# Queries of an attention block by seven quarter products: Strassen's algorithm for a second projection of a Trainium2 kernel

## The chip, the core and the metric

The kernel runs on one core of one Trainium2 chip. The metric is the device time in microseconds (us) of one execution. A core has five engines that run their own instruction queues in order and meet at semaphores: TensorE (PE, matrix products, with its weight loads shown as PEld), VectorE (DVE), ScalarE (ACT), GpSimd (POOL) and SyncE (SP, which issues DMAs). [...] All data here is 32-bit float, and each product that the program asks for is two matmul instructions and two weight loads in the trace.

## What is computed

One transformer block with adaptive layer norm, for two batches of 1024 tokens, 256 wide. The attention has 16 heads of 128, rotary positions and a causal mask; the second half is a gated feed-forward layer with dequantized weights.

```python
h = _layernorm(x) * (1 + ca) + sa
def proj(W, bias): return (h @ W + bias).reshape(b, n, 16, 128).transpose(0, 2, 1, 3)
q, k, v = proj(Wq, bq) * scale, proj(Wk, bk), proj(Wv, bv)
q, k = apply_rotary(pos, q), apply_rotary(pos, k)     # t*cos + rotate_half(t)*sin
sim = where(causal, -big, einsum('bhid,bhjd->bhij', q, k))
out = einsum('bhij,bhjd->bhid', softmax(sim), v)
x = x + ga * (out @ Wo + bo)
h = _layernorm(x) * (1 + cb) + sb
x = x + gb * down(silu(gate(h)) * up(h))
```

The projections q, k and v are each [1024 x 256] times [256 x 2048] per batch. The scale is folded into the softmax.

## The kernel before, in words

**Units.** The work is cut into 32 units, one for each batch b, group g of two heads, and head h in the group. Unit n is even for the first head of a group and odd for the second. A unit has eight turns i, one for each tile of 128 queries. The loop over units and turns writes the order of every queue out by hand: no scheduler moves anything, so each engine meets its instructions in the order of the program.

**One turn.** In turn i of unit n the program issues, in this order: the output projection of an earlier unit (`shared_out`, L622 to L634: one product "py" on PE, then an addition to x on DVE, L632); the scores of query tile i against (i+1)*128 keys (L542, "ps" on PE), then on DVE the mask and the row maximum (L545); the DVE transposition of the probabilities of the turn before (`turned`, L576, with DMAs after turns 3 and 7); the exponential on ACT (L562); `release()`, which issues the second halves of rotations that were begun in the turn before; then the projections that this turn has been given, the products of probabilities and values of the unit before (L603, "po" on PE, in turns 0, 6 and 7), and `extras`, where single jobs are placed by unit and turn.

**Queries and keys.** `project_qk` (L490 to L521) makes 512 tokens of one head: two products of 512 columns that add up in a PSUM bank, one for each half of the 256 inputs. Then come the rotation's parts: two ACT instructions read the bank crosswise into r1 (L511), POOL multiplies r1 by the sine table (L512); in the next turn DVE computes (bank + bias) * cosine (L515) and POOL adds r1 (L518). It is called in turns 1, 3, 4 and 5 of each unit for the next unit: query block 0, key block 0, query block 1, key block 1.

**Values.** From group 2 of the first batch on, 14 groups in all, `value_step` (L453 to L488) makes the values of both heads of a group from seven products of quarters instead of eight (Strassen's algorithm). The quarters are 512 tokens by 128 inputs, and 128 inputs by the 128 columns of one head. POOL forms sums of the token quarters once for each batch (`token_sum`) and, for each group, four sums of the weight quarters, in place and in one small tile (`weight_sums`, L440 to L451). Each product lies in one PSUM bank; ACT copies two of the seven to "snap" tiles, DVE adds five to snap tiles or values, and POOL adds two more times. Steps 1 to 3 are in turns 0 and 2 of an odd unit (for the next group), steps 4 to 7 in turns 0, 2 and 3 of the even unit that follows.

**Buffers.** Two PSUM banks ("ps_a") serve all projections in turn, one bank serves py, two pairs of banks serve the scores. Queries, keys, values and each of the weight tiles have two buffers, r1 has two.

Of the kernel before, what the change touches and what calls it, by code (L numbers as in the profile page):

```python
# [23 lines left out]
HG = 2  # L24
# [3 lines left out]
QB = 512  # L28
# [9 lines left out]
def adaln_block(ctx: ExitStack, tc: tile.TileContext, a, cos_d, sin_d, out):  # L38
    nc = tc.nc
    pool = lambda name, bufs, **k: ctx.enter_context(tc.tile_pool(name=name, bufs=bufs, **k))  # L40

    const = pool("const", 1)
# [4 lines left out]
    ps_a = pool("ps_a", 2, space=PSUM)  # L47
# [35 lines left out]
    def warm_up(tiles):  # L83
# [22 lines left out]

    modT = const.tile([P, 4, KC, B], F32, name="modT")
    gate = {
        (n, b): const.tile([P, D], F32, name=f"g{n}{b}") for n in ("a", "b") for b in range(B)
    }  # L110
    bo_bc = const.tile([P, D], F32, name="bo_bc")
    bvacc = const.tile([P, D], F32, name="bvacc")
# [33 lines left out]

    def gate_rows(n):

        for b in range(B):
            row = grow_d["ab".index(n), b : b + 1, :]  # L150
            nc.sync.dma_start(gate[n, b], row.to_broadcast([P, D]))
# [51 lines left out]
    wpool = pool("w", 2)  # L203
    vpool = pool("v", 2)
    qkpool = pool("qk", 2)
# [3 lines left out]
    tpool = pool("t", 1)  # L209
# [176 lines left out]
    gbo = {}  # L386

    def bias_row():

        pb = ps_a.tile([P, 512], F32, tag="a", name="pbias")  # L390
        nc.tensor.matmul(pb[:, :D], ones, bvacc, start=True, stop=True)
        nc.vector.tensor_tensor(bo_bc, pb[:, :D], bo_bc, ALU.add)
        for b in range(B):
            gbo[b] = const.tile([P, D], F32, name=f"gbo{b}")
            nc.gpsimd.tensor_tensor(gbo[b], gate["a", b], bo_bc, ALU.mult)

    def add_bias(b, t):
# [3 lines left out]
    weights = {}  # L401
# [21 lines left out]
    tT = {}  # L423
# [13 lines left out]
        }[n]  # L437
        nc.gpsimd.tensor_tensor(tT[b, n], x0, x1, ALU.subtract)

    def weight_sums(b, g, n):  # L440

        w = weights[b, g]["v"]
        a11, a12, a21, a22 = (w[:, k, ts(h, DH)] for h in range(HG) for k in range(KC))
        if n == 0:
            s2 = tpool.tile([P, DH], F32, tag="ws", name=f"ws_{b}{g}")
            wsum[b, g] = (a21, s2, a11, a12)
            nc.gpsimd.tensor_tensor(a11, a11, a21, ALU.subtract)
            nc.gpsimd.tensor_tensor(s2, a22, a11, ALU.subtract)
        else:
            nc.gpsimd.tensor_tensor(a21, a21, a22, ALU.add)  # L450
            nc.gpsimd.tensor_tensor(a12, a12, wsum[b, g][1], ALU.subtract)  # L451

    def value_step(b, g, step):  # L453
        w = weights[b, g]["v"]
        quarter = lambda k, blk: hT[b, blk][:, k, :]
        if step == 1:
            vs[b, g] = vpool.tile([P, NT, HG * DH], F32, tag="v", name=f"v_{b}{g}")
            for n in (1, 2):
                snap[n] = tpool.tile([P, QB], F32, tag=f"s{n}", name=f"snap{n}_{b}{g}")
        part = lambda h, blk: vs[b, g][:, ts(blk, QB // P), ts(h, DH)]  # L460
        tiles = lambda t: t.rearrange("p (t d) -> p t d", d=DH)

        def product(tokens, wq):
            bank = ps_a.tile([P, 512], F32, tag="a", name=f"pv{step}_{b}{g}")
            for r in range(QB // P):
                nc.tensor.matmul(bank[:, ts(r, P)], tokens[:, ts(r, P)], wq, start=True, stop=True)  # L466
            return bank

        add = lambda eng, to, x0, x1: eng.tensor_tensor(to, x0, x1, ALU.add)  # L469
        if step == 1:  # L470
            nc.scalar.copy(snap[1], product(quarter(0, 0), w[:, 0, ts(0, DH)]))
        elif step == 2:
            bank = product(quarter(1, 0), w[:, 1, ts(0, DH)])
            add(nc.vector, part(0, 0), tiles(bank), tiles(snap[1]))
        elif step == 3:
            add(nc.vector, snap[1], product(tT[b, 2], wsum[b, g][1]), snap[1])
        elif step == 4:
            bank = product(quarter(1, 1), wsum[b, g][3])
            add(nc.vector, part(0, 1), tiles(bank), tiles(snap[1]))
        elif step == 5:  # L480
            nc.scalar.copy(snap[2], product(tT[b, 1], wsum[b, g][0]))  # L481
            add(nc.gpsimd, part(0, 1), part(0, 1), tiles(snap[2]))
        elif step == 6:
            add(nc.vector, snap[1], product(tT[b, 3], wsum[b, g][2]), snap[1])
            add(nc.gpsimd, part(1, 1), tiles(snap[1]), tiles(snap[2]))
        else:
            bank = product(tT[b, 4], w[:, 1, ts(1, DH)])
            add(nc.vector, part(1, 0), tiles(bank), tiles(snap[1]))  # L488

    def project_qk(u, s, n):  # L490

        b, g, h = u
        head = g * HG + h
        if n == 0:
            qks[u, s] = qkpool.tile([P, S], F32, tag=f"{s}T", name=f"{s}T_{b}{g}{h}")
        dst = qks[u, s]
        pq = ps_a.tile([P, 512], F32, tag="a", name=f"p{s}_{b}{g}{h}{n}")
        for k in range(KC):
            nc.tensor.matmul(  # L499
                pq,  # L500
                weights[b, g][s][:, k, ts(h, DH)],
                hT[b, n][:, k, :],
                start=(k == 0),
                stop=(k == KC - 1),
            )
        c = (R_BQ if s == "q" else R_BK) + head
        sl, half = ts(n, QB), DH // 2

        r1 = rot.tile([P, QB], F32, tag="r1", name=f"r1_{s}{b}{g}{h}{n}")
        for to, of in ((slice(0, half), slice(half, DH)), (slice(half, DH), slice(0, half))):  # L510
            nc.scalar.activation(r1[to], pq[of], AF.Identity, bias=cols[of, c : c + 1])  # L511
        nc.gpsimd.tensor_tensor(r1, r1, sin_t[:, sl], ALU.mult)  # L512

        def rest():
            nc.vector.scalar_tensor_tensor(  # L515
                dst[:, sl], pq, cols[:, c : c + 1], cos_t[:, sl], ALU.add, ALU.mult
            )
            nc.gpsimd.tensor_tensor(dst[:, sl], dst[:, sl], r1, ALU.add)  # L518


        held.append(rest)  # L521
# [232 lines left out]
    N = len(units)  # L754

    def extras(n, i):
# [8 lines left out]
            gate_b()  # L765
        if n == 6 and i == 3:
            gate_b_turn()
        if n == 7 and i == 3:
            gate_rows("b")

        if n in (2, 15) and i in (0, 1, 3):
            for m in {0: (1, 2), 1: (3,), 3: (4,)}[i]:
                token_sum(n // 15, m)
        if n > 2 and n % 2 and i in (0, 3) and n + 1 < N:
            weight_sums(*units[n + 1][:2], i // 3)

        if n == 2 and i == 7:
            ffn_scale_load()
# [38 lines left out]
        if n == 20:  # L817
            add_bias(1, i)

    filler = (0, 1, 3, 4, 5, 6)  # L820

    def shared_out(s, late=False):
# [3 lines left out]
    with tc.manual_schedule():  # L826
# [52 lines left out]
        for n, u in enumerate(units):  # L879
            b, g, h = u  # L880
            prev = units[n - 1] if n else None
            nxt = units[n + 1] if n + 1 < N else None
            nb, ng = (b, g + 1) if g + 1 < NG else (b + 1, 0)
            more = nb < B
            for i in range(NT):

                shared_out(8 * n + i - 13)
                if owed:
                    owed.pop()()
                ps, nmax = score(u, i)  # L890
                if n > 2 and h == 0 and i == 3:
                    value_step(b, g, 7)
                if i >= 1:
                    turned(u, i - 1)
                elif prev:
                    turned(prev, NT - 1)
                expo(u, i, ps, nmax)
                release()
                if i in (1, 3, 4, 5) and nxt:
                    project_qk(nxt, *{1: ("q", 0), 3: ("k", 0), 4: ("q", 1), 5: ("k", 1)}[i])  # L900
                if i in (6, 7) and prev:
                    values(prev, 1, 4 * (i - 6), 4 * (i - 5))
# [12 lines left out]
                if n == 0 and i in (6, 7):  # L915
                    project_v(0, 1, 2 * (i - 6))
                if not nxt and i in filler:
                    hidden(0, 0, filler.index(i), late=False, hold=True)

                if prev and i == (0 if n > 2 else 2):  # L920
                    values(prev, 0, 0, 4)
                extras(n, i)
                if i == 7 and h == 1:
                    if more:
                        load_out(nb, ng)
                    if n + 3 < N:
                        load_proj(*units[n + 3][:2])
# [122 lines left out]
```

## Time and profile before

| what | us |
|---|---|
| median of 3 runs | 1061.07 (1060.88 to 1061.3) |
| the profiled execution | 1061.52 |
| its span, from the first to the last instruction | 1059.7 |
| PE busy (share of the span) | 1055.0 (100%) |
| DVE busy | 701.0 (66%) |
| ACT busy | 491.3 (46%) |
| POOL busy | 468.5 (44%) |
| granted TensorE clock, mean | 1.000 |

"Busy" is the union of an engine's instructions in the profiled execution. Matmuls are pipelined, so the records of neighbours overlap; what one costs in a stream is read from start to start in the timeline. The trace names instructions by line, engine, operation and tiles ("qT<-pq,cols,cos_t" writes qT from pq, cols and cos_t). A number of microseconds in square brackets is idle time of the engine before an instruction, with what released it.

### The profile page before, as it was taken

What the parts mean: (1) busy time and instruction counts of PE and PEld (TensorE: products, weight loads), DVE (VectorE), ACT (ScalarE), POOL (GpSimd) and SP (SyncE); (2) the same over time, 40 slices, a digit from 0 to 9 for tenths busy, and PEclk for the clock granted to TensorE, in tenths of its full rate; (3) what the DMA queues carried; (4) which work ended last, traced back from release to release, by engine and by line L of the source; (5) the groups of instructions that cost most, each with busy time, mean ns of one, the idle gap of its engine ahead of it and who ended that gap; (6) DMA issues with size and microseconds to landing.
All of it is one profiled execution on the core that took longest, in us unless ns stands there. A gap on an engine that the chain in (4) does not pass through costs nothing.

```text
span 1059.7 us, 13263 instructions
## 1 busy us (share of the span) xinstructions
PE 1055.0 (100%) x3834; PEld 638.4 (60%) x3834; DVE 701.0 (66%) x1523; ACT 491.3 (46%) x930; POOL 468.5 (44%) x461
## 2 busy tenths in 40 slices
PE   9999999999999999999999999999999999999998
PEld 5655566566666665665666666666565666555747
DVE  5667776777777776766676666666777866545331
ACT  5644444454445454444554444454454554562110
POOL 5755464645353554855644544434444544200100
PEclk9999999999999999999999999999999999999999
DMA  5466646666565646565565656454555657423201
GB/s 191 91 173 161 155 112 153 148 148 150 125 157 117 147 112 155 112 152 120 117 148 113 147 113 152 107 144 97 144 112 128 144 132 171 107 59 71 70 0 40
DMA packets 68379, 132.34 MB, mean 125 GB/s; under 512 B 19366, under 2 KB 23476, under 8 KB 68308
## 3 DMA queue, kind: packets, MB, share of 16 engines
q1 hardware_dynamic: 66060, 126.17, 50.6%
q10 hardware_dynamic: 2168, 5.20, 1.5%
q8 instruction: 31, 0.51, 0.2%
q14 instruction: 40, 0.33, 0.1%
q0 software_dynamic: 80, 0.13, 0.1%
HBM read 25.52 MB, written 2.10 MB: 26 GB/s over the span
## 4 chain that ended last, share of the span: by engine, by line
PE 99%; DVE 0%; issue 0%; POOL 0%; POOLq 0%
PE po L603 23%; PE ps L542 23%; PE py L629 10%; PE pq L499 10%; PE pk L499 10%; PE pv L466 8%; PE pgu L658 7%; PE pd L716 2%; PE pv L411 1%; PE pd_0w L716 1%; PE pd_1w L716 1%; PE warm_ps L85 0%; PE ptx_a L254 0%; PE pd L705 0%; PE pm L122 0%; DVE wupT L318 0%
## 5 line engine op out<-in xcount | busy, mean ns | idle before, releaser
L562 ACT ACTIVATE p<-ps,nmax 128x128 f32<-128x128 f32 (+7 forms) x256 | 190.3, 743 | 353.9 <-DVE nmax L545 353.6
L542 PE MATMUL ps<-kT,qT 128*128 128x512 f32 (+3 forms) x768 | 289.6, 486 | 0.0
L603 PE MATMUL po<-pT,v 128*128 128x512 f32 (+3 forms) x768 | 263.7, 486 | 0.2 <-DMA pT<-t 0.2
L545 DVE CUSTOM_DVE_ANT_0 ps<-ps,mask 128x128 f32<-128x128 f32 (+7 forms) x256 | 195.1, 762 | 100.5 <-PE ps L542 100.1
L632 DVE SCALAR_TENSOR_TENSOR x<-py,rden,x 128x256 f32<-128x256 f32 x256 | 122.2, 479 | 179.7 <-PE py L629 176.3
L603 PEld LDWEIGHTS po<-pT,v 128*128 128x128 f32 x768 | 143.6, 190 | 122.5 <-issue 93.5
L576 DVE STREAM_TRANSPOSE t<-p 128x128 f32<-128x128 f32 (+7 forms) x256 | 197.9, 773 | 5.3 <-DMA pT<-t 3.0
L542 PEld LDWEIGHTS ps<-kT,qT 128*128 128x128 f32 x768 | 145.8, 190 | 77.4 <-issue 63.4
L512 POOL TENSOR_TENSOR r_q<-r_q,sin_t 128x512 f32<-128x512 f32 x64 | 82.4, 1287 | 162.4 <-ACT r_q L511 161.0
L629 PE MATMUL py<-wo,o 128*128 128x256 f32 x512 | 151.8, 381 | 0.3 <-DVE x L632 0.3
L629 PEld LDWEIGHTS py<-wo,o 128*128 128x128 f32 x512 | 90.0, 191 | 77.5 <-issue 49.1
L499 PE MATMUL pq<-hT,wq 128*128 128x512 f32 x256 | 120.5, 593 | 0.0
L499 PE MATMUL pk<-hT,wk 128*128 128x512 f32 x256 | 120.3, 592 | 0.0
L512 POOL TENSOR_TENSOR r_k<-r_k,sin_t 128x512 f32<-128x512 f32 x64 | 81.7, 1277 | 47.0 <-ACT r_k L511 46.8
L518 POOL TENSOR_TENSOR kT<-kT,r_k 128x512 f32<-128x512 f32 x64 | 81.2, 1269 | 42.2 <-DVE kT L515 36.4
L511 ACT ACTIVATE r_q<-pq,cols 64x512 f32<-64x512 f32 x128 | 87.6, 684 | 23.5 <-PE pq L499 19.9
L518 POOL TENSOR_TENSOR qT<-qT,r_q 128x512 f32<-128x512 f32 x64 | 81.8, 1278 | 27.1 <-DVE qT L515 24.6
L511 ACT ACTIVATE r_k<-pk,cols 64x512 f32<-64x512 f32 x128 | 87.6, 684 | 10.7 <-PE pk L499 7.0
L499 PEld LDWEIGHTS pk<-hT,wk 128*128 128x128 f32 x256 | 47.5, 190 | 41.4 <-issue 34.9
L499 PEld LDWEIGHTS pq<-hT,wq 128*128 128x128 f32 x256 | 46.1, 190 | 32.8 <-issue 30.3
L611 ACT COPY o<-po 128x512 f32<-128x512 f32 x64 | 37.3, 582 | 59.5 <-PE po L603 59.5
L469 POOL TENSOR_TENSOR v<-v,snap 128x512 f32<-128x512 f32 x14 | 17.7, 1265 | 93.2 <-ACT snap L481 93.2
(135 smaller groups left out, 967.5 us busy)
## 6 DMA issues: line engine op xcount, KB each, us to landing
pT<-t SPq DMA_DIRECT2D x512, 128.0 KB, 2.4
pT<-t SPq DMA_DIRECT2D x512, 64.0 KB, 2.0
wq<-in_Wq SPq DMA_DIRECT2D x16, 256.0 KB, 3.1
wk<-in_Wk SPq DMA_DIRECT2D x16, 256.0 KB, 4.1
wv<-in_Wv SPq DMA_DIRECT2D x16, 256.0 KB, 4.1
wo<-in_Wo SPq DMA_DIRECT2D x16, 256.0 KB, 3.0
out<-yo SPq DMA_DIRECT2D x15, 128.0 KB, 1.7
x<-in_x ACTq DMA_DIRECT2D x4, 256.0 KB, 3.1
```

The source lines that it names most:

```text
L466: nc.tensor.matmul(bank[:, ts(r, P)], tokens[:, ts(r, P)], wq, start=True, stop=True)
L499: nc.tensor.matmul(pq, weights[b, g][s][:, k, ts(h, DH)], hT[b, n][:, k, :], start=(k == 0), stop=(k == KC - 1),)
L511: nc.scalar.activation(r1[to], pq[of], AF.Identity, bias=cols[of, c : c + 1])
L512: nc.gpsimd.tensor_tensor(r1, r1, sin_t[:, sl], ALU.mult)
L518: nc.gpsimd.tensor_tensor(dst[:, sl], dst[:, sl], r1, ALU.add)
L542: nc.tensor.matmul(ps[:, c:e], qT[:, ts(i, P)], kT[:, c:e], start=True, stop=True)
L545: nc.vector.tensor_tensor_reduce(ps[:, :L], ps[:, :L], mask[:, NT - 1 - i :, :].rearrange("p t k -> p (t k)"), -SCALE, FLT_MAX, ALU.add, A ...
L562: nc.scalar.activation(p[:, :L], ps[:, :L], AF.Exp, bias=nmax, scale=-1.0, accum_out=dens[u][:, i : i + 1])
L576: nc.vector.transpose(t32[blk][:, :, j, : i + 1, :].rearrange("p c k b -> p k c b"), p[:, : (i + 1) * P].rearrange("p (k c a) -> p k c a", ...
L603: nc.tensor.matmul(po[:, off * P :], vs[b, g][:, k, ts(h, DH)], pT[:, off:, :, k, :], start=(k == 0), stop=(k == last),)
L629: nc.tensor.matmul(py[:, :D], outs[u][:, ts(t, P)], weights[b, g]["o"][:, h, :], start=True, stop=True)
L632: nc.vector.scalar_tensor_tensor(x[b][:, t, :], py[:, :D], rdens[u][:, t : t + 1], x[b][:, t, :], ALU.mult, ALU.add)
```

## The change

For the same 14 groups, queries are made by the seven quarter products too. `value_step` becomes `set_step`, which serves both: an even unit n > 2 makes the values of its own group, an odd unit n > 2 the queries of both heads of the next group. One step is in each of turns 0, 1, 2, 4, 5, 6 and 7, after the exponential. `project_qk` stays for keys (turns 3 and 5) and for the first units.

A query quarter is finished in the query tile itself, in SBUF. The rotation (now a function of its own, `rotary`) is then applied in place: it is put in a list `due` by the step that completes a quarter, begun in the next turn after `release()`, and its second half, DVE and POOL, is released in the turn after that. Its lines are those of L506 to L521; where its source was a PSUM bank, it is now a part of the query tile. Quarters are completed in steps 2, 5, 6 and 7.

The weight sums are issued at the end of turns 0 and 2 of each such unit, behind everything else that the turn gives to POOL but `extras`. Queries have three buffers. For the room, the gate rows of the second half go into a weight buffer (and are loaded in unit 30 instead of 7), and the bias rows are kept in place of two others.

```diff
     def gate_rows(n):
+        if n == "b":
+            t = wpool.tile([P, KC, HG * DH], F32, tag="wq", name="gb")
+            for b in range(B):
+                gate["b", b] = t[:, b, :]
...
+        gbo.update({0: bvacc, 1: bo_bc})
         for b in range(B):
-            gbo[b] = const.tile([P, D], F32, name=f"gbo{b}")
             nc.gpsimd.tensor_tensor(gbo[b], gate["a", b], bo_bc, ALU.mult)
...
-    def value_step(b, g, step):
-        w = weights[b, g]["v"]
+    due = []
+
+    def set_step(b, g, name, step):
+        w = weights[b, g][name]
...
+        if name == "q" and step in (1, 6):
+            h = step // 6
+            qks[(b, g, h), "q"] = qkpool.tile([P, S], F32, tag="qT", name=f"qT_{b}{g}{h}", bufs=3)
...
+            part = lambda h, blk: qks[(b, g, h), "q"][:, ts(blk, QB)]
...
         def product(tokens, wq):
...
+                nc.tensor.matmul(bank, wq, tokens, start=True, stop=True)
             return bank
 
+        def done(h, blk):
+            if name == "q":
+                due.append(lambda: rotary((b, g, h), "q", blk, part(h, blk)))
+
         if step == 1:
             nc.scalar.copy(snap[1], product(quarter(0, 0), w[:, 0, ts(0, DH)]))
         elif step == 2:
             bank = product(quarter(1, 0), w[:, 1, ts(0, DH)])
             add(nc.vector, part(0, 0), tiles(bank), tiles(snap[1]))
+            done(0, 0)
         elif step == 3:
+            add(nc.vector, snap[1], product(tT[b, 2], s2), snap[1])
         elif step == 4:
+            bank = product(quarter(1, 1), s4)
             add(nc.vector, part(0, 1), tiles(bank), tiles(snap[1]))
         elif step == 5:
+            nc.scalar.copy(snap[2], product(tT[b, 1], s1))
             add(nc.gpsimd, part(0, 1), part(0, 1), tiles(snap[2]))
+            done(0, 1)
         elif step == 6:
+            add(nc.vector, snap[1], product(tT[b, 3], s3), snap[1])
             add(nc.gpsimd, part(1, 1), tiles(snap[1]), tiles(snap[2]))
+            done(1, 1)
         else:
             bank = product(tT[b, 4], w[:, 1, ts(1, DH)])
             add(nc.vector, part(1, 0), tiles(bank), tiles(snap[1]))
+            done(1, 0)
...
-        if n == 7 and i == 3:
+        if n == 30 and i == 3:
             gate_rows("b")
...
-        if n > 2 and n % 2 and i in (0, 3) and n + 1 < N:
-            weight_sums(*units[n + 1][:2], i // 3)
...
+    STEPS = {0: (1,), 1: (2,), 2: (3,), 4: (4,), 5: (5,), 6: (6,), 7: (7,)}
...
-                if n > 2 and h == 0 and i == 3:
-                    value_step(b, g, 7)
...
                 expo(u, i, ps, nmax)
                 release()
-                if i in (1, 3, 4, 5) and nxt:
+                while due:
+                    due.pop(0)()
+
+                setted = n > 2 and (not h or more) and ((nb, ng, "q") if h else (b, g, "v"))
+                if setted and i in STEPS:
+                    for step in STEPS[i]:
+                        set_step(*setted, step)
+                if i in (1, 3, 4, 5) and nxt and (i % 2 == 1 and i > 1 or n < 3):
                     project_qk(nxt, *{1: ("q", 0), 3: ("k", 0), 4: ("q", 1), 5: ("k", 1)}[i])
...
-                if n > 2 and (h == 0 or more) and i in (0, 2):
-                    vg = (nb, ng) if h else (b, g)
-                    for step in {(1, 0): (1, 2), (1, 2): (3,), (0, 0): (4, 5), (0, 2): (6,)}[h, i]:
-                        value_step(*vg, step)
...
                 if prev and i == (0 if n > 2 else 2):
                     values(prev, 0, 0, 4)
+                if setted and i in (0, 2):
+                    weight_sums(*setted, i // 2)
                 extras(n, i)
```

More of the change, by code (lines that the diff above doesn't have):

```diff
@@ L108, in adaln_block @@
     gate = {
-        (n, b): const.tile([P, D], F32, name=f"g{n}{b}") for n in ("a", "b") for b in range(B)
+        ("a", b): const.tile([P, D], F32, name=f"ga{b}") for b in range(B)
     }
@@ L438, in token_sum, with weight_sums @@
         nc.gpsimd.tensor_tensor(tT[b, n], x0, x1, ALU.subtract)
-    def weight_sums(b, g, n):
-        w = weights[b, g]["v"]
+    def weight_sums(b, g, name, n):
+        w = weights[b, g][name]
         a11, a12, a21, a22 = (w[:, k, ts(h, DH)] for h in range(HG) for k in range(KC))
         if n == 0:
-            s2 = tpool.tile([P, DH], F32, tag="ws", name=f"ws_{b}{g}")
-            wsum[b, g] = (a21, s2, a11, a12)
+            s2 = tpool.tile([P, DH], F32, tag="ws", name=f"ws{name}_{b}{g}")
+            wsum[b, g, name] = (a21, s2, a11, a12)
             nc.gpsimd.tensor_tensor(a11, a11, a21, ALU.subtract)
@@ L450, in weight_sums @@
             nc.gpsimd.tensor_tensor(a21, a21, a22, ALU.add)
-            nc.gpsimd.tensor_tensor(a12, a12, wsum[b, g][1], ALU.subtract)
-    def value_step(b, g, step):
-        w = weights[b, g]["v"]
+            nc.gpsimd.tensor_tensor(a12, a12, wsum[b, g, name][1], ALU.subtract)
+    due = []
+    def set_step(b, g, name, step):
+        w = weights[b, g][name]
         quarter = lambda k, blk: hT[b, blk][:, k, :]
         if step == 1:
-            vs[b, g] = vpool.tile([P, NT, HG * DH], F32, tag="v", name=f"v_{b}{g}")
+            if name == "v":
+                vs[b, g] = vpool.tile([P, NT, HG * DH], F32, tag="v", name=f"v_{b}{g}")
@@ L458, in value_step @@
             for n in (1, 2):
-                snap[n] = tpool.tile([P, QB], F32, tag=f"s{n}", name=f"snap{n}_{b}{g}")
-        part = lambda h, blk: vs[b, g][:, ts(blk, QB // P), ts(h, DH)]
-        tiles = lambda t: t.rearrange("p (t d) -> p t d", d=DH)
-        def product(tokens, wq):
-            bank = ps_a.tile([P, 512], F32, tag="a", name=f"pv{step}_{b}{g}")
-            for r in range(QB // P):
-                nc.tensor.matmul(bank[:, ts(r, P)], tokens[:, ts(r, P)], wq, start=True, stop=True)
-            return bank
+                snap[n] = tpool.tile([P, QB], F32, tag=f"s{n}", name=f"snap{name}{n}_{b}{g}")
@@ new lines, in set_step @@
+        if name == "q" and step in (1, 6):
+            h = step // 6
+            qks[(b, g, h), "q"] = qkpool.tile([P, S], F32, tag="qT", name=f"qT_{b}{g}{h}", bufs=3)
+        if name == "v":
+            part = lambda h, blk: vs[b, g][:, ts(blk, QB // P), ts(h, DH)]
+            tiles = lambda t: t.rearrange("p (t d) -> p t d", d=DH)
+        else:
+            part = lambda h, blk: qks[(b, g, h), "q"][:, ts(blk, QB)]
+            tiles = lambda t: t
+        def product(tokens, wq):
+            bank = ps_a.tile([P, 512], F32, tag="a", name=f"p{name}{step}_{b}{g}")
+            if name == "v":
+                for r in range(QB // P):
+                    nc.tensor.matmul(
+                        bank[:, ts(r, P)], tokens[:, ts(r, P)], wq, start=True, stop=True
+                    )
+            else:
+                nc.tensor.matmul(bank, wq, tokens, start=True, stop=True)
+            return bank
@@ L469, in value_step @@
+        def done(h, blk):
+            if name == "q":
+                due.append(lambda: rotary((b, g, h), "q", blk, part(h, blk)))
         add = lambda eng, to, x0, x1: eng.tensor_tensor(to, x0, x1, ALU.add)
+        s1, s2, s3, s4 = wsum.get((b, g, name), (None,) * 4)
         if step == 1:
@@ L474, in value_step @@
             add(nc.vector, part(0, 0), tiles(bank), tiles(snap[1]))
+            done(0, 0)
         elif step == 3:
-            add(nc.vector, snap[1], product(tT[b, 2], wsum[b, g][1]), snap[1])
+            add(nc.vector, snap[1], product(tT[b, 2], s2), snap[1])
         elif step == 4:
-            bank = product(quarter(1, 1), wsum[b, g][3])
+            bank = product(quarter(1, 1), s4)
             add(nc.vector, part(0, 1), tiles(bank), tiles(snap[1]))
         elif step == 5:
-            nc.scalar.copy(snap[2], product(tT[b, 1], wsum[b, g][0]))
+            nc.scalar.copy(snap[2], product(tT[b, 1], s1))
             add(nc.gpsimd, part(0, 1), part(0, 1), tiles(snap[2]))
+            done(0, 1)
         elif step == 6:
-            add(nc.vector, snap[1], product(tT[b, 3], wsum[b, g][2]), snap[1])
+            add(nc.vector, snap[1], product(tT[b, 3], s3), snap[1])
             add(nc.gpsimd, part(1, 1), tiles(snap[1]), tiles(snap[2]))
+            done(1, 1)
         else:
@@ L488, in value_step @@
             add(nc.vector, part(1, 0), tiles(bank), tiles(snap[1]))
+            done(1, 0)
     def project_qk(u, s, n):
         b, g, h = u
-        head = g * HG + h
         if n == 0:
-            qks[u, s] = qkpool.tile([P, S], F32, tag=f"{s}T", name=f"{s}T_{b}{g}{h}")
-        dst = qks[u, s]
+            qks[u, s] = qkpool.tile(
+                [P, S], F32, tag=f"{s}T", name=f"{s}T_{b}{g}{h}", bufs=3 if s == "q" else 2
+            )
         pq = ps_a.tile([P, 512], F32, tag="a", name=f"p{s}_{b}{g}{h}{n}")
@@ L505, in project_qk, with rotary @@
             )
+        rotary(u, s, n, pq)
+    def rotary(u, s, n, pq):
+        b, g, h = u
+        head = g * HG + h
+        dst = qks[u, s]
         c = (R_BQ if s == "q" else R_BK) + head
```

## The prediction, as it went on record

> **What bounds the kernel now.** I read the shares of the engines first, then the chain of work that ended last.
>
> ```profile
> PE 1055.0 (100%) x3834; PEld 638.4 (60%) x3834; DVE 701.0 (66%) x1523; ACT 491.3 (46%) x930; POOL 468.5 (44%) x461
> ...
> PE 99%; DVE 0%; issue 0%; POOL 0%; POOLq 0%
> ```
>
> The chain is PE's own stream for 99% of the span: PE waits for nobody, so a product less is time gained, and a wait that PE does not have today is time lost in full. What a product costs is read from start to start in PE's timeline, here of the first turns of an even unit:
>
> ```profile
> 357.99 0.60 PE L629 MATMUL py<-wo,o 128*128 128x256 f32 x2
> 358.43 0.39 PE L542 MATMUL ps<-kT,qT 128*128 128x128 f32 x2
> 358.65 1.06 PE L466 MATMUL pv<-wv,hT 128*128 128x128 f32 x8
> 359.54 1.06 PE L466 MATMUL pv<-wv,tT 128*128 128x128 f32 x8
> 360.44 2.32 PE L603 MATMUL po<-pT,v 128*128 128x512 f32 x8
> 362.59 0.60 PE L629 MATMUL py<-wo,o 128*128 128x256 f32 x2
> 363.03 0.59 PE L542 MATMUL ps<-kT,qT 128*128 128x256 f32 x2
> 363.46 1.88 PE L499 MATMUL pq<-hT,wq 128*128 128x512 f32 x4
> 365.18 0.59 PE L629 MATMUL py<-wo,o 128*128 128x256 f32 x2
> ```
>
> Columns: start, length, engine, line, tiles, count. Two products of 512 columns (x4) take 365.18 - 363.46 = 1.72, so one takes 0.86; a quarter product for values (x8) takes 0.89; py 0.44; scores 0.22 per 128 keys; po in turn 0 takes 2.15.
>
> **What goes.** A group's queries took 8 such products and take 7: 14 x 0.858 = **12.0 us off PE**. This is the whole gain.
>
> **What is added elsewhere, by rows of the value steps.** For each of 14 groups: five DVE additions of 0.68, two ACT copies of 0.58, two POOL additions of 1.27 and four POOL weight sums of 0.455 (together 48 us of DVE, 16 of ACT, 61 of POOL). The shares stay below 75%, and in sum nothing becomes the bound. By turn, from start to start, DVE is longer than PE only in turn 1 of an even unit (reciprocal 0.25, x 0.42, maximum 0.41, transposition 0.23, L515 0.60, addition 0.60: 2.5 against 1.7) and in turn 4 (x 0.42, maximum 0.75, transposition 0.63, L515 0.63, addition 0.60: 3.0 against 2.4). It catches up in turns 3 and 5, and PE's next py finds x done. What has to be read is the order of the queues at the places where PE takes something from POOL: weight sums s2 (for step 3, turn 2) and s4 (for step 4, turn 4). Today `weight_sums` has nothing ahead of it when it is wanted. In the new order it stands behind the rotations.
>
> **One row decides how long these are.** DVE's second half of a rotation (L515) read PSUM and cosines; for Strassen queries it reads the query tile in SBUF and cosines, two SBUF operands. The only such DVE form with POOL at work beside it is L318, here on DVE and then on POOL:
>
> ```profile
> 193.96 1.67 DVE L318 SCALAR_TENSOR_TENSOR wgateT<-raw,s_bc 128x640 f32<-128x640 int32 x1
> 195.55 0.47 DVE L632 SCALAR_TENSOR_TENSOR x<-py,rden,x 128x256 f32<-128x256 f32 x1
> ...
> 193.68 1.27 POOL L518 TENSOR_TENSOR qT<-qT,r_q 128x512 f32<-128x512 f32 x1
> 194.91 1.85 POOL L469 TENSOR_TENSOR v<-snap,snap 128x512 f32<-128x512 f32 x1
> ```
>
> L318 takes 0.81 in the minimum of its row, here 1.67: it ends 0.68 after the POOL instruction that was running when it began. And POOL's next, usually 1.27, takes 1.85: it starts to work when DVE is done. The two exclude one another and alternate. [...] For 512 columns I take L318's minimum less 128 columns, 0.68, of which 0.60 go by before DVE's next instruction. [...]
>
> **Even units, step 3.** Times count from the start of py of turn 0.
> - PE: py 0.44, scores 0.22, step 1 0.89, po 2.15: turn 1 at 3.70. Then 0.44 + 0.43 + 0.89: turn 2 at 5.46. Then 0.44 + 0.64: step 3 would start at **6.54**.
> - From the odd unit before come three rotations of queries: (0,1) to be added by POOL, (1,1) to be multiplied and added, (1,0) whole. DVE in turn 0 does x, row maximum, and the transposition of the last turn, which ends at 2.41 (in today's trace 357.99 + 2.41 = 360.40). POOL: add (0,1) 0.2 to 1.4, multiply (1,1) 1.4 to 2.7. DVE's half of (1,1) wants to begin at 2.41, waits until 2.7, ends at 3.3. POOL adds it from 3.45 (0.14 after, as L518 follows L515) to 4.7, and multiplies (1,0) from 4.7 to 5.95 (ACT is done with it at 3.5).
> - DVE's half of (1,0) is in turn 1 behind x, maximum and transposition, at 5.4; it waits until 5.95 and ends at 6.55. The weight sums, behind POOL's multiplication, wait for DVE: first 6.55, s2 0.53 later at 7.08, ends **7.53**.
> - PE takes 0.05 from the end of what it waits for to its weight load, and loses about 0.1 for the load (377.67 to 377.72 and 0.11, where py waits for x today). Step 3 starts at 7.69: **a stall of 1.15**.
>
> Without the exclusion DVE's halves start at 2.41 and 5.36, POOL's chain is 3.26, 4.49, 5.73, s2 ends at 6.72, and the stall is 0.35.
>
> **Odd units, step 4.** PE would start it at 11.84 (turn 2 with a 512-column product at 5.39, turn 3 at 7.32, turn 4 at 10.33, plus 0.43 + 1.08). Step 2's sum is in the tile at 6.2; its rotation is begun in turn 2 behind the exponential: maximum 6.66, exponential 7.38, ACT free 8.06, two ACT halves to 9.44, POOL's multiplication 9.52 to 10.79. DVE's half wants 9.91, waits, and is done at 11.4. Only then the weight sums of turn 2: 11.35 and 0.41 later, s4 ends 12.2, step 4 starts at 12.35: **a stall of 0.5**. Without the exclusion s4 ends at 11.65, no stall.
>
> **Units with layer-norm work on DVE** (9 to 12 and 25 to 28): `ln_stats` adds 0.52 to turns 1 to 4, `ln_scale` and `ln_move` about 1.0. Today they already push x to the edge (PE loses 0.1 at 341.58 and 377.72). With DVE fuller in turns 1, 2 and 4, I take 0.25 more each, 2 us in all; bounds 0 and 0.6 each (5 us), the latter one DVE addition late.
>
> **Costed at nothing.** Banks: each step's bank is read a turn before its next use; step 5 takes the bank of key block 0, released by L515 in turn 4, 0.4 before. Third query buffer: no wait for a buffer of the unit in use. Gate rows: two loads of 3.1 us to landing in unit 30, turn 3, on SP's queue, read in unit 31, turn 1, some 25 us later; were the cover gone, one wait of at most 3. Their weight buffer was last read in unit 29. Bias rows: the same two POOL instructions. The values' later steps: blocks 0 and 1 of the first head are done in turns 2 and 5, read in the next unit. A turn's score reads only finished columns: block 1 of the first head is added by 1.4 of the next unit and read in turn 4, if waits go by ranges; L447 today starts when the first product is done with a part of the weight tile and the second is still reading another (331.11, with step 2 on PE until 331.76), so they do.
>
> **The sum.** -12.0 + 14 x 1.15 + 14 x 0.5 + 2 = -12.0 + 16.1 + 7.0 + 2.0 = **+13.1**: 1061.5 becomes 1074.6 by the profiled execution, which is 0.45 above the median of the runs: 1074. Bounds of each stall, for this case alone: 0.9 and 0.25 (DVE granted before POOL once less) and 1.6 and 0.8 (one more DVE instruction ahead), so 1065 to 1084.
>
> **Rivals.**
> - *Only the queue, no exclusion for this form* (13%): 14 x 0.35 = 4.9 and 1.5 for layer norm: 1061.1 - 12.0 + 6.4 = 1055.5, faster. For it: L318's source is int32, the new one is not. Against: the row maximum over two SBUF operands (L182) also goes from 420 to 1484 ns.
> - *All of it hidden* (10%): PE gains its 12.0, 1049. For it: POOL is 44% busy and idle in most of turns 1 and 2 today; some 1.1 us less in the chain of the even units is enough. Against: each link is a measured row.
> - *The scores wait for the whole query tile* (7%): score 0 would wait for POOL's add of block 1, until 1.4 instead of 0.44, and shift all behind it: 14 x 1.0 more, 1088. It decides as soon as waits go by tiles.
> - That the change does not do what it says is out: eight product calls of a group are replaced by seven.
>
> **How the numbers follow.** Forecast 70%, the rivals 13, 10 and 7. Faster by over 0.2% (what a measurement of this kernel can tell from no change): the first two rivals and a little of the forecast's lower end, 0.24; slower 0.73; between 0.03. The range reaches to the first rival and leaves out the second and the third: 1055 to 1084; the forecast's own is 1065 to 1084.
>
> **What would show it.** PE's weight loads of step 3 idle about 1.1 in each even unit, released by POOL's sum, and of step 4 about 0.5 in each odd one; L515 on queries with rows up to 2 us, L518 and L512 up to 1.9; PE busy some 12 us less, the span longer. I am wrong if L515 stays near 0.7, or if POOL reaches s2 by 6.5.

## The result, and the profile after

The changed kernel takes 1075.59 us (median; 1061.06 before): a ratio of 1.0131 with a 95% interval of 1.0112 to 1.0151. Forecast were 1074, slower, in a range of 1055 to 1084. Run again beside the experiments it took 1074.73, ratio 1.012 (1.0105 to 1.0135). The profile shown here is of that second run (e0_again, the same kernel, span 1072.5), since the execution first profiled had a mean granted TensorE clock of 0.557 and took 1853 us.

The shares of the engines and the chain that ended last, after:

```profile
PE 1056.7 (99%) x3806; PEld 633.5 (59%) x3806; DVE 748.6 (70%) x1593; ACT 508.9 (47%) x958; POOL 537.0 (50%) x545
...
PE 71%; issue 12%; POOL 6%; DVE 6%; ACT 2%; DMA 1%; SPq 0%; DVEq 0%; POOLq 0%; ACTq 0%
```

The chain was PE for 99% and is PE for 71% now: it leaves PE for POOL, DVE and ACT in many places. PE has 28 matmul instructions less (14 products), and yet its busy time is 1.7 longer, because a matmul whose operand comes late is recorded some 0.10 longer (e0_again: 697 ns at most against a median of 592 in the rows of L486, 377 against 275 in those of L482), and the record of the matmul before it covers a part of the wait (by my estimate some 0.16: 0.59 is recorded for 512 columns, and 0.429 go by from start to start). The view of waits of PE itself names who holds it (columns: who waits, for whom, us in total, times, longest):

```profile
PE pq L486 <- POOL wq L456: 4.9, 14, 0.6
PE po L639 <- ACT o L647: 2.9, 14, 0.2
PE py L665 <- DVE x L668: 1.7, 3, 0.6
...
PE pv L482 <- POOL wsv L453: 0.6, 1, 0.6
```

L486 with L456 is step 4 of the queries behind s4, fourteen times, as forecast. L482 with L453 is step 3 of the values behind s2. The second line, the products of probabilities and values behind a copy on ACT, was not forecast.

These totals are only part of the loss, since the weight load waits first (PEld's own waits are, in all, 10.1 for s2, 7.6 for s4, 10.2 for the copy of po and 16.1 for x). So I took PE's time from start to start in the timeline of units 0 to 30 and subtracted what an instruction of that width takes in an undisturbed stream (0.429 for 512 columns, 0.322, 0.216 and 0.11 for 384, 256 and 128). I call the rest, where it is over 0.02, **PE's loss**: 1.7 us before, 26.2 after. Units without layer-norm work and other single jobs are called plain. Against the 12.0 that the products save, 24.5 more loss is +12.5, and the spans differ by 1072.5 - 1059.7 = 12.8. So the account closes. By place:

| PE waits in | for | us in all | in a plain unit | forecast |
|---|---|---|---|---|
| even units, turn 0, po | ACT's copy that frees the bank of po | 6.6 | 0.47 | none |
| even units, turn 2, step 3 | POOL's s2 | 5.2 | 0.34 | 1.15 |
| even units, turn 3, py | DVE's x | 2.4 | 0 | (layer norm) |
| odd units, turn 4, step 4 | POOL's s4 | 8.7 | 0.48 | 0.5 |
| other places | x 1.4; the rest in po and in steps 5 and 6 | 3.3 | 0 | (layer norm) |

An even unit in detail. PE's timeline, from py of turn 0:

```profile
656.68 0.60 PE L665 MATMUL py<-wo,o 128*128 128x256 f32 x2
657.11 0.38 PE L578 MATMUL ps<-kT,qT 128*128 128x128 f32 x2
657.33 1.06 PE L482 MATMUL pv<-wv,hT 128*128 128x128 f32 x8
658.60 2.42 PE L639 MATMUL po<-pT,v 128*128 128x512 f32 x8 [0.21 <-ACT o L647]
660.86 0.60 PE L665 MATMUL py<-wo,o 128*128 128x256 f32 x2
661.29 0.59 PE L578 MATMUL ps<-kT,qT 128*128 128x256 f32 x2
661.72 1.05 PE L482 MATMUL pv<-wv,hT 128*128 128x128 f32 x8
662.61 0.60 PE L665 MATMUL py<-wo,o 128*128 128x256 f32 x2
663.05 0.81 PE L578 MATMUL ps<-kT,qT 128*128 128x384 f32 x2
663.93 0.82 PE L482 MATMUL pv<-wsv,tT 128*128 128x128 f32 x5
```

po starts at 658.60 instead of 657.33 + 0.89 = 658.22. Step 3 could start at 663.05 + 0.64 = 663.69 and starts at 663.93. Each loses 0.10 more behind its late first matmul, which makes the 0.47 and the 0.34 of the table. The same microseconds on DVE, ACT and POOL (three answers, in this order):

```profile
657.92 1.24 DVE L612 STREAM_TRANSPOSE t<-p 128x1024 f32<-128x1024 f32 x1
659.09 0.87 DVE L551 SCALAR_TENSOR_TENSOR qT<-qT,cols,cos_t 128x512 f32<-128x512 f32 x1
...
662.56 1.00 DVE L551 SCALAR_TENSOR_TENSOR qT<-qT,cols,cos_t 128x512 f32<-128x512 f32 x1
...
656.48 1.45 ACT L547 ACTIVATE r_q<-qT,cols 64x512 f32<-64x512 f32 x2
657.96 0.58 ACT L647 COPY o<-po 128x512 f32<-128x512 f32 x1
...
656.90 1.28 POOL L554 TENSOR_TENSOR qT<-qT,r_q 128x512 f32<-128x512 f32 x1 [2.99 <-DVE qT L551]
658.14 1.26 POOL L548 TENSOR_TENSOR r_q<-r_q,sin_t 128x512 f32<-128x512 f32 x1
660.10 1.26 POOL L554 TENSOR_TENSOR qT<-qT,r_q 128x512 f32<-128x512 f32 x1 [0.70 <-DVE rden L662]
661.33 1.27 POOL L548 TENSOR_TENSOR r_q<-r_q,sin_t 128x512 f32<-128x512 f32 x1
662.55 0.46 POOL L452 TENSOR_TENSOR wv<-wv 128x128 f32<-128x128 f32 x1
663.09 0.78 POOL L453 TENSOR_TENSOR wsv<-wv 128x128 f32<-128x128 f32 x1
```

POOL's chain is the one of the prediction: add, multiply, add, multiply, two weight sums; s2 ends at 663.87, 7.19 after the start of py (forecast 7.53). It is 0.34 earlier because one of the two sums does not wait: DVE's half, forecast at 5.4 behind py, starts at 5.88, when the multiplication has all but ended, and the first sum goes ahead of it. ACT's rotation stands ahead of the copy of po, which is done at 658.54, when PE has wanted the bank for 0.3. The last weight sum takes 0.78 instead of 0.455, because DVE's half, which ends 0.55 after the first one, stands between.

And an odd unit, step 4 (PE, then POOL, then DVE):

```profile
638.59 1.24 PE L578 MATMUL ps<-kT,qT 128*128 128x512 f32 x4
640.03 1.12 PE L486 MATMUL pq<-hT,wq 128*128 128x512 f32 x2 [0.20 <-POOL wq L456]
...
637.44 1.27 POOL L548 TENSOR_TENSOR r_q<-r_q,sin_t 128x512 f32<-128x512 f32 x1 [6.87 <-ACT r_q L547]
638.66 0.90 POOL L455 TENSOR_TENSOR wq<-wq 128x128 f32<-128x128 f32 x1
639.52 0.45 POOL L456 TENSOR_TENSOR wq<-wq,wsq 128x128 f32<-128x128 f32 x1
...
637.75 1.50 DVE L551 SCALAR_TENSOR_TENSOR qT<-qT,cols,cos_t 128x512 f32<-128x512 f32 x1
```

DVE's half begins inside POOL's multiplication and takes 1.50; the weight sum behind it takes 0.90, half of it waiting for DVE; step 4 is due at 638.59 + 1.08 = 639.67 and starts at 640.03; with 0.10 more behind its first matmul the loss is 0.48.

### The profile page after: what moved, and what is told of

Read it like the earlier page. It is cut to its first block, busy times and chain, and to the rows that moved or that the text cites. A ratio compares the mean times of both kernels' runs of the same rounds, so it can differ in the third digit from the quotient of the medians.

```text
span 1851.7 us, 13478 instructions
## 1 busy us (share of the span) xinstructions
PE 1847.4 (100%) x3806; PEld 822.4 (44%) x3806; DVE 752.1 (41%) x1593; ACT 513.1 (28%) x958; POOL 524.7 (28%) x545
## 4 chain that ended last, share of the span: by engine, by line
PE 100%; issue 0%; DVE 0%; POOL 0%; POOLq 0%
PE ps L578 24%; PE po L639 24%; PE py L665 11%; PE pk L528 11%; PE pq L486 8%; PE pv L482 8%; PE pgu L694 7%; PE pd L752 2%; PE pq L528 1%; PE pv L416 1%; PE pd_0w L752 1%; PE pd_1w L752 1%; PE warm_ps L85 0%; PE pd L741 0%; PE ptx_a L259 0%; PE pm L122 0%
## 5 line engine op out<-in xcount | busy, mean ns | idle before, releaser
L578 PE MATMUL ps<-kT,qT 128*128 128x512 f32 (+3 forms) x768 | 493.6, 775 | 0.0
L639 PE MATMUL po<-pT,v 128*128 128x512 f32 (+3 forms) x768 | 461.7, 774 | 0.0
L639 PEld LDWEIGHTS po<-pT,v 128*128 128x128 f32 x768 | 174.3, 232 | 292.2 <-issue 282.7
L578 PEld LDWEIGHTS ps<-kT,qT 128*128 128x128 f32 x768 | 174.3, 227 | 220.5 <-issue 182.5
L665 PE MATMUL py<-wo,o 128*128 128x256 f32 x512 | 245.7, 582 | 0.0
L528 PE MATMUL pk<-hT,wk 128*128 128x512 f32 x256 | 209.5, 967 | 0.0
L482 PEld LDWEIGHTS pv<-wv,tT 128*128 128x128 f32 x336 | 68.5, 246 | 30.3 <-issue 27.8
L547 ACT ACTIVATE r_q<-qT,cols 64x512 f32<-64x512 f32 x112 | 80.6, 719 | 2.1
L486 PE MATMUL pq<-tT,wq 128*128 128x512 f32 x84 | 72.9, 967 | 0.0
L482 PE MATMUL pv<-wv,hT 128*128 128x128 f32 x336 | 72.9, 390 | 0.0
```

Source lines behind the costliest of these rows:

```text
L486: nc.tensor.matmul(bank, wq, tokens, start=True, stop=True)
L528: nc.tensor.matmul(pq, weights[b, g][s][:, k, ts(h, DH)], hT[b, n][:, k, :], start=(k == 0), stop=(k == KC - 1),)
L578: nc.tensor.matmul(ps[:, c:e], qT[:, ts(i, P)], kT[:, c:e], start=True, stop=True)
L639: nc.tensor.matmul(po[:, off * P :], vs[b, g][:, k, ts(h, DH)], pT[:, off:, :, k, :], start=(k == 0), stop=(k == last),)
L665: nc.tensor.matmul(py[:, :D], outs[u][:, ts(t, P)], weights[b, g]["o"][:, h, :], start=True, stop=True)
```

## The experiments

Theory A is the prediction's. B and C are its rivals, stated with the first experiment; D came after the first four results.

**e0_again**: no edit. 

> The changed kernel once more, for a profile at the full clock. Theory A (weight sums on POOL come late behind the rotations, and DVE and POOL exclude one another while DVE reads two SBUF operands): 1074 to 1076 us; PE's step 3 of each even unit starts about 1.15 us late and step 4 of each odd unit about 0.5 late, released by POOL. Theory B (the queue order alone, no exclusion): the same time cannot come out, step 3 would be 0.35 late. Theory C (DVE's fuller turns: py waits for x): the waits stand before py, released by DVE's x, some 1.7 us for two units.

Measured: 1074.73. Step 4 as expected, step 3 late by 0.34, which is B's number; but s2 itself ends at 7.19, nearer to A's 7.53 than to the 6.72 without the exclusion, and PE had lost 0.47 ahead of it. C's place, py, is late only in units with more work on DVE. So none of the three stands as written.

**e1_sums_first**, the weight sums ahead of the due rotation:

```diff
-                while due:
-                    due.pop(0)()
+                ready = due[:]
+                due.clear()
...
+                if setted and i in (0, 2):
+                    weight_sums(*setted, i // 2)
+                for begin in ready:
+                    begin()
...
-                if setted and i in (0, 2):
-                    weight_sums(*setted, i // 2)
```

> Only an order is changed: in turns 0 and 2 the weight sums are issued right behind the step, ahead of the rotation that was due, so that POOL meets them one multiplication earlier. Theories A and B: s2 ends near 5.6 and s4 near 8 us of their units, ahead of PE, and both stalls go: 1075.6 - 14 x 1.15 - 14 x 0.5 = 1052.5 us (1050 to 1056). Theory C: no change, 1074 to 1076.

Measured: 1075.42, 0.7 more than e0_again, so nothing gained: A's and B's expectation was wrong by 23. The waits for s2 and s4 are gone, and PE's loss is 28.5 instead of 26.2: 11.5 of it now in turn 3 of even units, at py. The timelines of POOL and then DVE show where they went:

```profile
662.95 1.27 POOL L548 TENSOR_TENSOR r_q<-r_q,sin_t 128x512 f32<-128x512 f32 x1
...
663.25 1.52 DVE L551 SCALAR_TENSOR_TENSOR qT<-qT,cols,cos_t 128x512 f32<-128x512 f32 x1
664.69 0.68 DVE L493 TENSOR_TENSOR v<-pv,snapv 128x512 f32<-128x512 f32 x1
665.29 0.47 DVE L668 SCALAR_TENSOR_TENSOR x<-py,rden,x 128x256 f32<-128x256 f32 x1
```

POOL's multiplication, put behind the sums, ran from 662.95 to 664.22; DVE's half met it and took 1.52 instead of 1.00, and x of turn 2, two instructions behind, ended at 665.76, after PE was due to start py of turn 3 at 664.38 + 0.89 = 665.27. The wait for POOL had become a wait for DVE.

**e2_psum_source**, DVE's half of a query rotation with one SBUF operand:

```diff
+            if late:
+                m = min(4, now[1] + 1)
+                some = now[0][:, : m * P].unsqueeze(1).to_broadcast([P, 4 // m, m * P])
+                parts = lambda t: t[:, sl].rearrange("p (a b) -> p a b", a=4 // m)
...
+                nc.vector.scalar_tensor_tensor(
+                    parts(dst), some, 0.0, parts(cos_t), ALU.mult, ALU.add
+                )
```

`now[0]` is the PSUM tile with the scores of the turn, and `late` marks the rotations of query quarters.

> The order stays. DVE's half of a query rotation reads the scores of the turn in PSUM (times zero) and the cosines, instead of the query quarter in SBUF: the same DVE length and place in every queue, one SBUF operand instead of two. The quarter's cosine product and bias are left out of the result. Theory A: no exclusion, s2 ends at 6.7 instead of 7.5 and s4 at 11.65: 1075.6 - 14 x 0.8 - 14 x 0.5 = 1057.4 us (1054 to 1061). Theory B and theory C: no change, 1074 to 1076.

Measured: 1071.02, 3.7 less than e0_again, where A had 18 and B and C none. The exclusion itself is plain. The rows of this DVE form in e0_again, for keys (from PSUM) and for quarters of queries (from SBUF), and then in e2 (min, median and max in ns):

```profile
L551 DVE SCALAR_TENSOR_TENSOR kT<-pk,cols,cos_t x64: 701/708/751, 17.2 to 914.5; 128x512 f32<-128x512 f32 x64
L551 DVE SCALAR_TENSOR_TENSOR qT<-qT,cols,cos_t x56: 708/929/1775, 107.4 to 898.3; 128x512 f32<-128x512 f32 x56
```

```profile
L559 DVE SCALAR_TENSOR_TENSOR qT<-ps,cos_t x56: 647/691/693, 108.8 to 895.8; 128x512 f32<-128x512 f32 x56
```

With two SBUF operands it takes up to 1775; with one, the same instruction in the same execution stays at 751 and the changed one at 693. The waits for s4 fell from 8.7 to 2.3 and for s2 from 5.2 to 3.5; but po kept its 6.6, and x in front of py rose (even units 2.4 to 3.7, odd ones in turn 5 from 0.8 to 2.9).

What the exclusion costs in time, e2 does not show, because its edit brought a wait of its own (columns of the row: busy us, mean ns, then idle time of DVE before it, with its releaser):

```profile
L559 DVE SCALAR_TENSOR_TENSOR qT<-ps,cos_t 128x512 f32<-128x512 f32 x56 | 38.1, 681 | 18.7 <-ACT p L610 18.6
```

The half now waits for the exponential of the turn on ACT, 18.6 us in all; in e0_again it does not. In a plain even unit it starts 6.37 after py of turn 0 (660.38 after 654.01) instead of 5.88, the half ahead of it 2.85 instead of 2.41, and s2 ends at 7.09, where A had 6.7 and PE wants it at 7.01. So 3.7 is what the removal brings together with this wait.

**e34_raw_both**, steps 3 and 4 without the sums:

```diff
-            add(nc.vector, snap[1], product(tT[b, 2], s2), snap[1])
+            add(nc.vector, snap[1], product(tT[b, 2], w[:, 1, ts(1, DH)]), snap[1])
...
-            bank = product(quarter(1, 1), s4)
+            bank = product(quarter(1, 1), w[:, 1, ts(1, DH)])
```

> Steps 3 and 4 take an unsummed quarter of the weights, so PE waits for no weight sum there; all sums are still made, in the same order. The values and queries lack the two sums. Theories A and B: the two stalls go and nothing else changes: 1052.5 us (1050 to 1056). Theory C: no change, 1074 to 1076.

Measured: 1067.11, 7.6 less. This is the clearest answer: the sums being late cost 7.6, not 23, and not the 13.9 that the table has at steps 3 and 4 either. Those are gone, and 5.9 have come up elsewhere. Of the loss 18.2 are left: po 6.7, py in even units 4.8, py and step 5 in turn 5 of odd units 5.3. From here on theory D: *several queues end at nearly the same time, all behind the same rotations, and PE meets whichever is last.*

**e12_both**: the edits of e1 and e2 together. 

> Both edits of before at once: the weight sums ahead of the due rotation on POOL, and DVE's half of a query rotation with one operand in PSUM (its quarter is left out of the result). Theory D, formed from the trace of the changed kernel: three queues end at almost the same time in turns 0 to 2 of an even unit, and each waits for the same rotations: ACT's copy that frees the bank of po (PE loses 0.47), POOL's s2 (0.34 more) and DVE's x in front of py (next, within some 0.1 to 0.5); in odd units s4 (0.48). Here s2, s4 and x come in time and only the bank is late: 14 x 0.47 = 6.6 and some 4 to 6 for the units with layer-norm work are left of 26: 1060 us (1058 to 1063). If the waits were independent terms, e1 (+0.7) and e2 (-3.7) would add up: 1071 to 1072.

Measured: 1071.17. D's number (1060) was wrong and the sum of the two edits was right, though for no reason of its own: the loss is e2's 23.2, with other places. s2 and s4 cost nothing, po its 6.7, and py 7.3 in even and 5.6 in odd units. In turn 1 x was late once more, behind a DVE half that had waited for the exponential as in e2:

```profile
660.75 0.69 DVE L559 SCALAR_TENSOR_TENSOR qT<-ps,cos_t 128x512 f32<-128x512 f32 x1 [0.44 <-ACT p L610]
```

**e6_all_three**: as e12_both, and in turn 7 the rotation begun behind the copy of po.

```diff
+                for begin in ready if i < 7 else ():
+                    begin()
...
                 if i in (6, 7) and prev:
                     values(prev, 1, 4 * (i - 6), 4 * (i - 5))
+                for begin in ready if i == 7 else ():
+                    begin()
```

> As e12_both, and in turn 7 the due rotation is begun behind the copy of po on ACT, so that the bank is free in time. Theory D: nothing is late in even units without layer-norm work, and the whole product comes out: 1061.1 - 12.0 + 4 to 6 = 1054 us (1052 to 1057). If the product does not come out as time of PE at all: near e12_both, 1060.

Measured: 1065.3, 5.9 less than e12_both, but 11 over D's 1054. The 6.6 of po go in full (6.7 to 0 in even units), which no edit before had touched; but 17.3 of loss are left. By unit: 0.3 in every plain even one and none in plain odd ones, and 14 in units 3, 5, 9 to 12 and 25 to 28, those with layer-norm work or with other single jobs on DVE or POOL, most of it (some 11) at py behind x. e2's wait is in this kernel too (18.7 us of DVE), so it is not known how much of the 17.3 the edit itself made.

**e5_copy_first**: the edit that e6 adds, alone. 

> The changed kernel with only the last edit: in turn 7 the due rotation is begun behind the copy of po on ACT. Theory D: the 0.47 for the bank go, but the rotation (1,1) is begun 1.2 us later on ACT, POOL's multiplication, DVE's half and s2 behind it too: s2 ends near 7.8 and step 3 waits 1.3 instead of 0.34. Slower than the changed kernel: 1074.7 + 14 x 0.5 = 1082 us (1077 to 1084). If the bank's wait is a term of its own: 1068.

Measured: 1087.61, 12.9 more than e0_again (expected 7). D's sign was right: the wait of po goes and step 3 waits 1.86 per even unit, 26.0 in all. It is more than 1.3 because DVE's half of (1,1) came 0.06 after POOL had started and waited for all of it (POOL, then DVE):

```profile
666.30 1.27 POOL L548 TENSOR_TENSOR r_q<-r_q,sin_t 128x512 f32<-128x512 f32 x1 [0.85 <-ACT r_q L547]
...
666.36 1.75 DVE L551 SCALAR_TENSOR_TENSOR qT<-qT,cols,cos_t 128x512 f32<-128x512 f32 x1
```

**f1_early**: all rotations of queries inside the odd unit.

```diff
+    QSTEPS = {0: (1, 2), 1: (3,), 2: (4, 5), 4: (6,), 5: (7,)}
...
+                steps = QSTEPS if h else STEPS
...
+                for m in ((0, 1) if h and i == 0 else (i // 2,) if not h and i in (0, 2) else ()):
+                    if setted:
+                        weight_sums(*setted, m)
...
+                for each in (*begun, *ready):
+                    each()
```

`begun` holds the second halves of the turn before, `ready` what is due.

> A version meant to be used, with the reference's whole result: odd units make queries in turns 0 (steps 1, 2), 1 (3), 2 (4, 5), 4 (6) and 5 (7), both pairs of weight sums in turn 0, and the halves of query rotations behind the turn's own step, so that all rotations of queries end inside the odd unit and nothing of them is in the first turns of the even one. Theory D: the waits of the even units go, and in odd units the sums are early; left are 4 to 8 us in units with layer-norm work and a wait of 1.3 at the change of batch: 1061.1 - 12.0 + 6 = 1055 us (1052 to 1060), faster than both kernels. If DVE's fill is the limit whatever the order: 1068 to 1075.

Measured: 1058.82, ratio 0.9973 (0.9964 to 0.9982): faster than before, 4 short of the expectation. Plain units lose nothing: from start to start the even one takes 0.75 less than before, the odd one 0.11 less, together 0.86, one product. The exclusion is there as before (the DVE half has a median of 1120 ns), but in plain units nothing that PE waits for stands behind it. The largest loss is in unit 15, 5.3, at the change of batch.

**f2_tokens**: the token sums of the second batch earlier (two at the end of unit 14, two in turns 0 and 1 of unit 15).

> f1_early with the token sums of the second batch earlier: the first two at the end of unit 14, the other two in turns 0 and 1 of unit 15, where the first such products now want them (f1 lost 5.3 us in unit 15: 1.4 before step 3, and 3.9 before step 7 and behind it, where PE ran at half its clock after it had idled). Theory D: that wait goes, the rest stays: 1058.8 - 5 = 1054 us (1052 to 1056). If the sums only push other work of POOL: 1056 to 1059.

Measured: 1054.19 (1062.31 before, beside it), ratio 0.9927 (0.9914 to 0.9939), as D expected. PE's loss is 5.3. Its chain is PE again for most of the span:

```profile
PE 1045.0 (99%) x3806; PEld 633.3 (60%) x3806; DVE 759.0 (72%) x1593; ACT 508.8 (48%) x958; POOL 541.7 (51%) x545
...
PE 94%; DVE 4%; DMA 1%; issue 0%; ACT 0%; SPq 0%; DVEq 0%; ACTq 0%
```

DVE, ACT and POOL are as busy as in the slower kernel, within 11 us of 1052; only the order differs.

**f3_late**: f2_tokens with step 7 of queries in turn 6 instead of 5 in units 11 and 27.

> f2_tokens with step 7 of the queries one turn later in units 11 and 27, where layer-norm work fills DVE and py of turn 6 waited 1.3 for x in each. Theory D: DVE has one addition less ahead of that x: up to 2.5 us less than f2_tokens, 1051.5 (1050.5 to 1054). If the wait moves one turn on: as f2_tokens.

Measured: 1059.74, 5.6 more than f2_tokens, where a gain was expected. In both units the wait before py of turn 6 grew from 1.4 to 2.3: PE had one product (0.86) less to do before it, and x came no sooner. And po in the next unit waited 1.3. Taking PE work out of a turn that DVE bounds only turned it into a wait. The loss in the two units and those behind them grew by 4.4; another 1.1 is in unit 2, ahead of the edit. The executions of f3_late spread from 1057.95 to 1063.37.

## Why the prediction was right, and which of its steps were not

- *A product costs 0.86, and 14 of them are 12.0 off PE*: right. f1 and f2 show the 0.86 in full in each pair of plain units.
- *PE waits for nobody today, so a new wait is lost in full*: right; the account of 12.0 saved and 24.5 lost closes to 0.3.
- *DVE and POOL exclude one another with two SBUF operands on DVE*: right, as read from L318. The form of the rotation with one operand in PSUM takes 702 to 752 ns in all 128 cases of before (L515) and 701 to 751 for the keys of e0_again; with two in SBUF it goes from 708 to 1775. The first rival (no exclusion for this form) is out by these rows, the second (all of it hidden, 1049) by the time, and the third by the score of turn 0, which starts 0.43 behind py (657.11), not 1.4.
- *Even units, step 3, a stall of 1.15*: the failed step. It measured 0.34. PE came 0.47 later than worked out, because "po 2.15" was taken to start on time. The chain on POOL was right to 0.34 (s2 at 7.19 instead of 7.53): the prediction let DVE's half go ahead of both sums, and with PE late it went between them. The two make the difference: 1.15 - 0.47 - 0.34 = 0.34.
- *Costed at nothing: banks*: failed. Only the two banks of the projections were followed. po has one bank, its copy on ACT stands behind the rotation that was moved ahead of it, and that costs 0.47 per even unit, 6.6 in all. Only the two edits that put the copy ahead of the rotation (e5, e6) take it away. The two places together were forecast at 1.15 and measured 0.81.
- *Odd units, step 4, 0.5*: right, 0.48 in plain units; 8.7 in all against 7.0, the rest mostly in units with layer-norm work.
- *Units with layer-norm work, 2 us, at most 5*: too small. Plain units account for 14 x 0.81 + 14 x 0.48 = 18.1 of the loss of 26.2; the 8.1 left, 6.4 more than before, lie in units 2, 3, 5, 9 to 12, 17, 18 and 25 to 28. The eight units that the term names lost some 0.6 each, its upper bound, where it took 0.25; the rest is in units that it left out.
- *The sum* came to 25.1 of waits where 24.5 were added. That is the right size from terms of which one was too large by 11, one missing by 7 and one short by 4, so that the forecast of 1074 came this close is luck. The range joins two sums: with the layer-norm term at 2 the bounds of the stalls give 1067 to 1085, with that term at its own bounds 1065 to 1088. PE's busy time was forecast some 12 lower and is 1.7 higher. What the sum does not say, and what I read out of it all the same in e1 and e34, is that a term is what its removal brings. e34 takes both waits for sums away and brings 7.6; e1 brings nothing.

What stays open: what the exclusion alone costs, since e2, e12 and e6 replaced it in part by a wait for the exponential; and how much of e6's remaining 14 us belongs to that wait, to DVE's work in those units and to POOL's, since no run took single jobs out of them.

## What to carry to other kernels

When a saving on the bounding engine is paid with work on others, follow every resource that the moved work touches, the copy that frees a one-bank accumulator among them (0.47 per even unit here), and expect several queues to end together: then the loss from the latest one is not what its removal brings (13.9 against 7.6 in e34), and only an order that takes the added work out of the tight turns altogether (f1 and f2) freed the saving. When an experiment swaps an operand, look at what its instruction waits for now: e2 took one wait away and brought another. Before changing a DVE instruction's source from PSUM to SBUF, see whether its other tensor is in SBUF too and what POOL does at that moment (up to 752 ns for the rotation here with one SBUF operand, up to 1775 with two). A version that is slower by 1.3% and one that is faster by 0.7% had the same instructions; so a bad result of a rearranged pipeline says little about the arithmetic it was made for.

## What the runs showed of the hardware that was not expected

In one execution TensorE's granted clock fell from 1.00 to 0.50 behind a wait of 2.0 us. In f1, unit 15, PE idled from 462.6 to 464.6, and in the 3.4 us that followed it was granted 0.59 at first and then 0.50 (PE's timeline, then windows; columns: window, its length, busy time and instructions of PE, PEld, DVE, ACT and POOL, granted clock, DMA share, GB/s):

```profile
464.62 2.01 PE L486 MATMUL pq<-tT,wq 128*128 128x512 f32 x2 [1.98 <-POOL tT L443]
466.43 2.73 PE L528 MATMUL pk<-hT,wk 128*128 128x512 f32 x4
...
462.60:464.60 2.00, 0.04 (x1) 0.00 (x0) 1.90 (x5) 0.00 (x0) 2.00 (x3) 1.00 0.43 98
464.60:465.30 0.70, 0.68 (x1) 0.44 (x2) 0.70 (x3) 0.16 (x1) 0.70 (x1) 0.59 0.41 94
465.30:466.00 0.70, 0.70 (x2) 0.34 (x1) 0.45 (x1) 0.70 (x2) 0.70 (x2) 0.50 0.50 114
466.00:467.00 1.00, 1.00 (x2) 0.34 (x1) 0.33 (x1) 0.14 (x2) 1.00 (x2) 0.50 0.55 125
467.00:468.00 1.00, 1.00 (x2) 0.34 (x1) 0.36 (x1) 0.00 (x0) 1.00 (x2) 0.50 0.05 8
468.00:468.50 0.50, 0.50 (x2) 0.19 (x1) 0.00 (x0) 0.00 (x0) 0.24 (x1) 0.86 0.49 111
```

So a wait of 2.0 cost 3.9 with what came behind it (PE's loss at these matmuls). Four of f1's ten executions have a mean clock of 0.998, as this one, and six 1.000, so by the means it does not come in each execution.

The same operations from SBUF instead of PSUM: DVE's half of a rotation has a minimum of 708 ns with two SBUF operands (e0_again) against 702 with one of them in PSUM (before), so it is no shorter; ACT's halves of query rotations take 717 to 723 ns instead of 682 to 690.
